# LoRA and paged attention in one kernel: a new order of loads, tables and fillers ahead of the steps, the inverse root ahead of the addition, and queries of step 1 and of the last step turned on TensorE

## The chip, the core and the metric

The kernel runs on one core of one Trainium2 chip. The metric is the device time of one launch in microseconds, as the median of several runs. Beside it stands one execution taken by the hardware profiler, which gives the span from the first to the last instruction and everything that is read from views of the profile.

## The reference, cut to what matters

All data are float32. There are 8 sequences of 128 tokens with 512 features. First each sequence goes through its own adapter weight, and the result is added; then attention over a paged cache is computed on the sum and added again.

```python
x = x + einsum('bsi,boi->bso', x, weight[adapter_ids])     # (8,128,512), adapters 512x512
# attention: 32 query heads, 8 key heads, D = 128, cache of 16 pages x 32 = 512 keys
q = rope(rmsnorm(x @ Wq.T) * q_norm_w)                     # rmsnorm per head
k = rope(rmsnorm(x @ Wk.T) * k_norm_w);  v = x @ Wv.T
scores = q @ [cached keys, k].T / sqrt(D)                  # 512 + 128 keys
scores = where(key number < cache_seqlens (cache part), scores, -1e30)
x = x + (softmax(scores) @ [cached values, v]) @ Wo.T
```

## The kernel before

**Steps.** The work is cut into 32 steps, `steps = [(g, b)]`: four groups g of 8 query heads and 2 key heads, and in each group the 8 sequences b. The projected weights of a group stay in SBUF for its 8 steps. Step i computes 8 heads; for each it does two score matmuls (`sc`, L891, 512 and 128 keys; each shows as two instructions in the profile), a masking and row-minimum operation on VectorE (L901), the exponential on ScalarE (L917), the scaling by the reciprocal on POOL (L966, `p<-p,rc`) and a turn of the probabilities.

**Fillers.** Between two heads, TensorE gets a share of other matmuls from the list `main`: the projections of step i+1 (`project`: `pj_kv`, and `pj_q` for each half of four query heads), `values(i-1, j)` (probabilities times values, `o<-pT`), and `output(i-1)` (`out<-w_o`). In the first group `lora_y` (`y`) and turns of x and of the adapter weight (`lw`) are added. The flag `early` puts the projections ahead of `values(i-1, 0)`; it holds for steps from 8 on. Short TensorE jobs that have a fixed place are in the table `turns_at`, filled with `at(i, head, early, job)`.

**Order.** The order of instructions is the order of the program text (`tc.manual_schedule()`); each engine and each DMA queue runs its own instructions in that order, and semaphores between them are derived from the tiles' buffers. So an instruction that waits holds up all that stand behind it on its engine or queue. SP's queue carries most transfers, ScalarE's queue weights, POOL's queue the gathers of cache pages (`kc`, `vc`) and of adapter weights (`raw_lora`, `lraw`).

**Two ways to turn a matrix.** Through DRAM: VectorE transposes 32x32 blocks, one DMA writes them out and a second reads them back in the right order (`send_q`: `xq<-tq`, then `qT<-xq`; `send_k`/`receive_k`: `xk`, `kT`; `send`/`receive`: `xp`, `pT`; the weights of groups 1 to 3: `xw`, `w`). Or on TensorE: four transposes into a PSUM buffer and a copy out (`turn_q`, `turn_weights`, `turn_x`, `turn_kc`, `turn_lora`). The queries of step 0 are turned on TensorE, those of steps 1 to 31 go through DRAM. PSUM has four buffers for these jobs and for projections (`ps_mm`), and two for scores (`ps_sc`).

**A query half.** When its projection ends, ScalarE takes the squares of its heads (L552), VectorE multiplies by the rotation tables (L557, L561), POOL adds the two products (L568), then adds epsilon to the square sums (L584) and takes the power -1/2 (L585, `rs`); ScalarE scales the four heads with it (L590), VectorE the keys (L593).

**Ahead of the steps.** Loads are issued from SP and ScalarE, the rotation tables are computed with the sine of ScalarE (`rope_tables`, L345 to L385), the row numbers of cache pages on VectorE (`row_numbers`, L278 to L322), and the weights of group 0, x of sequences 0 and 1 and their adapter weights are turned on TensorE, up to the output weights (`wt_o`, 32 transposes). The first score matmul follows.

Of the kernel before, what the change touches and what calls it, by code (L numbers as in the profile page):

```python
# [11 lines left out]
FP = mybir.dt.float32  # L12
# [6 lines left out]
P = 128  # L19
# [33 lines left out]
def lora_then_paged_attention(  # L53
# [51 lines left out]
    def load_x(b, eng=None):  # L105
# [7 lines left out]
    wn = const.tile([P, 2, D], FP, name="wn")  # L113
    nc.scalar.dma_start(out=wn[:, 0, :], in_=q_norm_w.partition_broadcast(P))
    nc.scalar.dma_start(out=wn[:, 1, :], in_=k_norm_w.partition_broadcast(P))
    bt_i = work.tile([P, 4, S], I32, tag="oT0", name="bt_i")
    bt_i = bt_i.rearrange("p a s -> p (a s)")[:, 0 : 4 * B * LC].rearrange("p (c q) -> p c q", q=4)
    nc.scalar.dma_start(
        out=bt_i.rearrange("p c q -> p (c q)"),
        in_=block_table.rearrange("b n -> (b n)").partition_broadcast(P),  # L120
    )
    par = const.tile([P, 1], I32, name="par")
    nc.gpsimd.iota(par, pattern=[[0, 1]], base=0, channel_multiplier=1)
    ident = const.tile([P, P], FP, name="ident")
    make_identity(nc, ident)

    lora_ix = const.tile([P, B], I32, name="lora_ix")
    nc.vector.scalar_tensor_tensor(
        out=lora_ix,
        in0=ids_i,  # L130
        scalar=float(HID // 4),
        in1=par.to_broadcast([P, B]),
        op0=ALU.mult,
        op1=ALU.add,
    )
    lora_rows = lora_w.rearrange("m (p j) i -> (m p) (j i)", j=4)

    def weight_rows(kind, g, n, m=1):  # L140
        if kind == "kv":
            src = wk if n < 2 else wv
            lo = g * GW + (n % 2) * P
            return src[lo : lo + m * P, :]
        if kind in ("q0", "q1"):
            lo = (g * GQ + 4 * int(kind[1])) * D + n * P
            return wq[lo : lo + m * P, :]
        half = int(kind[1])
        lo = (g * GQ + 4 * half) * D
        return wo[n * P : (n + m) * P, lo : lo + 4 * D]  # L150

# [14 lines left out]
    raw = {}  # L166


    first = {}
    for kind, pl, tag in (("kv", turned, "tp"), ("lora", turned, "tp"), ("q0", pts, "pT")):  # L170
        t = pl.tile([P, 4, REP, QK], FP, tag=tag, name=f"raw_{kind}")
        first[kind] = t.rearrange("p a r k -> p (a r k)")[:, 0 : 4 * HID]

    t = wts.tile([P, 4, 4, 4, Q4], FP, tag="o1", name="raw_q1")
    first["q1"] = t.rearrange("p n b c j -> p (n b c j)")

    def load_first(kind, n, m):
        nc.sync.dma_start(
            out=first[kind][:, n * 512 : (n + m) * 512].rearrange("p (n i) -> p n i", n=m),
            in_=weight_rows(kind, 0, n, m).rearrange("(n p) i -> p n i", p=P),  # L180
        )
        for k in range(n, n + m):
            raw[kind, 0, k] = first[kind][:, k * 512 : (k + 1) * 512]

# [10 lines left out]
    for i, (g, b) in enumerate(steps):  # L195
        if i == 0:
            at(i, 1, True, lambda: turn_x1(1))
            at(i, 3, False, lambda: turn_q(0, 1))
        at(i, 2, True, lambda i=i: turn_k(i, 1), 1)
# [18 lines left out]
    for g in range(1, G):  # L218
        before = 8 * B * (g - 1)
        for k, kind in enumerate(("kv", "q0", "q1")):  # L220
            for n in range(4):
                turn_when[before + 9 + 3 * (4 * k + n)] = len(turns_of)
                turns_of.append((kind, g, n))
                h = (2, 3, 5)[k] if g > 1 else (3, 4, 6)[k]
# [18 lines left out]
    load_first("kv", 0, 2)  # L243
    load_first("kv", 2, 2)
    load_first("q0", 0, 4)
    load_x(1)
    load_first("q1", 0, 4)
    load_x(2)

    for k in range(2):  # L250
        for n in range(4):
            t = (acc, x1T)[k][B - 4 + n]
            raw[f"o{k}", 0, n] = t if k == 0 else t.rearrange("p c s -> p (c s)")
            nc.sync.dma_start(out=raw[f"o{k}", 0, n], in_=weight_rows(f"o{k}", 0, n))
# [5 lines left out]
    inner = const.tile([P, 1], FP, name="inner")  # L260
    quad = const.tile([P, 1], FP, name="quad")
    for a in range(4):
        rows = slice(Q4 * a, Q4 * a + Q4)
        nc.gpsimd.iota(
            inner[rows, :],
            pattern=[[0, 1]],
            base=0,
            channel_multiplier=1,
            allow_small_or_imprecise_dtypes=True,
        )  # L270
        nc.gpsimd.memset(quad[rows, :], float(a))
# [3 lines left out]
    def row_numbers():  # L275
# [52 lines left out]
    len_f = const.tile([P, B], FP, name="len_f")  # L328

    key_no = const.tile([P, 4, LC, Q4], FP, name="key_no")  # L330
    nc.gpsimd.iota(
        key_no,
        pattern=[[1, 4], [P, LC], [4, Q4]],
        base=0,
        channel_multiplier=0,
        allow_small_or_imprecise_dtypes=True,
    )
    mhalf = const.tile([P, GQ + GK], FP, name="mhalf")
    nc.gpsimd.memset(mhalf, -0.5)
    masks = [const.tile([P, 4, NC, Q4], FP, name=f"mask_{n}") for n in range(2)]  # L340
    for m in masks:
        nc.gpsimd.memset(m[:, :, LC, :], 0.0)

    def rope_tables():
# [26 lines left out]
        nc.scalar.activation(cos, ang, AF.Abs)  # L371
        nc.vector.tensor_scalar(cos, cos, -1.0, math.pi / 2, ALU.mult, ALU.add)
        nc.scalar.activation(cos, cos, AF.Sin)


        nc.vector.tensor_scalar(wn[:, 0, :], wn[:, 0, :], -SCALE, None, ALU.mult)
# [664 lines left out]
```

## Time and profile before

| | us |
|---|---|
| median of 3 runs | 1244.26 (1242.14 to 1245.38) |
| profiled execution, its time | 1243.9 |
| profiled execution, its span | 1242.1 |
| TensorE matmuls busy | 1193.6 (96%) |
| VectorE busy | 752.9 (61%) |
| POOL busy | 670.5 (54%) |
| ScalarE busy | 527.5 (42%) |
| start to the first score matmul | 57.1 |
| mean granted TensorE clock | 0.986 |

Busy time of an engine is the union of its instructions; register work, waits and the issue of DMAs are not in it. In a row of groups or of the timeline, `out<-in` names the tiles; the bracket behind it gives the idle time of that engine just before the row and what ended it. PE is TensorE's matmul, PEld its weight load, DVE VectorE, ACT ScalarE, SPq and ACTq the issue of a DMA from that queue. The granted clock is a share of full speed.

### The profile page before, as it was taken

The numbers are of one execution on the slowest core, as the hardware profiler recorded it, in microseconds if no ns is written. First come the engines' busy times: TensorE is split into PE (matmuls) and PEld (weight loads), VectorE is DVE, ScalarE is ACT, GpSimd is POOL, SyncE is SP. The second block draws the span as 40 slices with busy tenths as digits, with TensorE's granted clock in tenths as the row PEclk, the third lists the DMA queues.
The fourth block names the chain that finished last, engine by engine and source line by source line (L and its number), as shares of the span: only waits on it lengthen the run. The fifth ranks groups of instructions, "written<-read, shape, count | busy, mean of one in ns | idle before, by whom it ended". The sixth has DMA issues, their size and how long they took to land.

```text
span 1242.1 us, 12908 instructions
## 1 busy us (share of the span) xinstructions
PE 1193.6 (96%) x3380; PEld 579.8 (47%) x3380; DVE 752.9 (61%) x1684; ACT 527.5 (42%) x1643; POOL 670.5 (54%) x763
## 2 busy tenths in 40 slices
PE   6788999999989999999999999999999999999988
PEld 4544444444434444444444444444444444444443
DVE  5264656565646667766666667666666655665731
ACT  3453444444434444444444444443444444444422
POOL 3354464446535566655655566655565556655440
PEclk9898999999999999999999999999999999999989
DMA  7246877786988898888999898888898897777761
GB/s 285 95 151 210 297 256 257 269 286 222 309 275 267 267 334 291 271 296 279 289 346 312 267 342 278 290 277 285 295 352 282 270 299 258 240 263 239 241 223 59
DMA packets 189592, 329.83 MB, mean 266 GB/s; under 512 B 13520, under 2 KB 108112, under 8 KB 180432
## 3 DMA queue, kind: packets, MB, share of 16 engines
q1 hardware_dynamic: 126256, 239.37, 57.6%
q10 hardware_dynamic: 49824, 47.69, 11.9%
q0 software_dynamic: 13440, 41.96, 9.9%
q8 instruction: 27, 0.44, 0.1%
q14 instruction: 45, 0.37, 0.1%
HBM read 196.06 MB, written 132.91 MB: 265 GB/s over the span
## 4 chain that ended last, share of the span: by engine, by line
PE 83%; DMA 10%; DVE 2%; POOL 2%; ACT 1%; issue 1%; ACTq 0%; SPq 0%; DVEq 0%; POOLq 0%
PE sc L891 20%; PE o L474 20%; PE pj_q L474 16%; PE out L474 14%; PE pj_kv L474 8%; DMA qT<-xq 3%; DMA xp<-tp 2%; PE y L474 2%; DMA w_q<-xw_q 2%; DMA xq<-tq 1%; PE lw L397 1%; DMA raw_lora<-in_L_cond_weight_dram,lora_ix 1%; DMA lraw<-in_L_cond_weight_dram,lora_ix 1%; PE x L397 1%; POOL rs L585 1%
## 5 line engine op out<-in xcount | busy, mean ns | idle before, releaser
L901 DVE CUSTOM_DVE_ANT_0 p<-sc,mask 128x640 f32<-128x640 f32 x256 | 210.7, 823 | 350.1 <-PE sc L891 349.5
L891 PE MATMUL sc<-kT,qT 128*128 128x512 f32 (+1 forms) x1024 | 323.5, 439 | 20.5 <-DMA qT<-xq 17.6
L917 ACT ACTIVATE p<-p,mn 128x640 f32<-128x640 f32 x256 | 211.5, 826 | 285.3 <-DVE mn L901 283.2
L891 PEld LDWEIGHTS sc<-kT,qT 128*128 128x128 f32 x1024 | 191.3, 192 | 251.4 <-issue 228.2
L966 POOL TENSOR_SCALAR p<-p,rc 128x640 f32<-128x640 f32 x252 | 201.7, 800 | 193.3 <-DVE rc L959 189.0
L474 PE MATMUL o<-pT,vc 128*128 128x512 f32 x512 | 241.1, 602 | 1.2 <-DMA pT<-xp 1.2
L474 PE MATMUL pj_q<-w_q,x1T 128*128 128x512 f32 x512 | 237.5, 593 | 0.4 <-DMA w_q<-xw_q 0.3
L752 DVE STREAM_TRANSPOSE tp<-p 128x640 f32<-128x640 f32 x252 | 210.7, 836 | 42.3 <-POOL p L966 42.0
L474 PE MATMUL out<-w_o,oT 128*128 128x512 f32 x512 | 235.0, 593 | 0.8 <-ACT oT L726 0.7
L590 ACT ACTIVATE q<-q,rs 128x128 f32<-128x128 f32 x256 | 81.9, 390 | 219.6 <-POOL rs L585 212.5
L520 POOL DMA_INDIRECT kc<-in_L_cond_k_cache_dram,key_ix x128 | 128.9, 1007 | 48.3 <-issue 30.4
L520 POOL DMA_INDIRECT vc<-in_L_cond_v_cache_dram,val_ix x128 | 129.1, 1008 | 35.7 <-issue 31.1
L568 POOL TENSOR_TENSOR q<-q,sw 128x512 f32<-128x512 f32 x64 | 81.8, 1279 | 103.4 <-DVE sw L561 103.1
L474 PEld LDWEIGHTS out<-w_o,oT 128*128 128x128 f32 x512 | 92.7, 190 | 95.7 <-issue 93.5
L474 PEld LDWEIGHTS o<-pT,vc 128*128 128x128 f32 x512 | 93.6, 194 | 92.8 <-issue 84.3
L474 PEld LDWEIGHTS pj_q<-w_q,x1T 128*128 128x128 f32 x512 | 92.5, 191 | 92.3 <-issue 90.1
L474 PE MATMUL pj_kv<-w_kv,x1T 128*128 128x512 f32 x256 | 118.0, 598 | 0.9 <-DVE x1T L399 0.9
L572 POOL TENSOR_TENSOR k<-sw 128x256 f32<-128x256 f32 x31 | 22.9, 740 | 140.8 <-PE kt L653 130.5
L552 ACT ACTIVATE sq<-pj_q 128x128 f32<-128x128 f32 x256 | 70.8, 277 | 48.4 <-PE pj_q L474 39.7
L585 POOL TENSOR_TENSOR rs<-ss,mhalf 128x6 f32<-128x6 f32 x64 | 76.7, 1198 | 5.3
L474 PEld LDWEIGHTS pj_kv<-w_kv,x1T 128*128 128x128 f32 x256 | 46.6, 193 | 46.8 <-issue 45.7
L474 PE MATMUL o<-pT,vn 128*128 128x512 f32 x128 | 65.4, 593 | 0.0
(110 smaller groups left out, 882.5 us busy)
## 6 DMA issues: line engine op xcount, KB each, us to landing
xp<-tp SPq DMA_DIRECT2D x63, 1280.0 KB, 5.7
pT<-xp SPq DMA_DIRECT2D x63, 1280.0 KB, 6.7
xk<-tk SPq DMA_DIRECT2D x31, 512.0 KB, 7.6
kT<-xk SPq DMA_DIRECT2D x62, 256.0 KB, 6.4
xq<-tq SPq DMA_DIRECT2D x62, 256.0 KB, 4.0
qT<-xq SPq DMA_DIRECT2D x62, 256.0 KB, 6.1
st_q<-in_L_cond_Wq_dram ACTq DMA_DIRECT2D x24, 256.0 KB, 4.2
xw_q<-tw_q ACTq DMA_DIRECT2D x24, 256.0 KB, 3.7
```

Of the source, the lines that this page charges most:

```text
L397: nc.tensor.transpose(t[:, j, :], blk, ident)
L474: nc.tensor.matmul(y[0], lhsT=lhsT, rhs=rhs, start=(k == 0), stop=(k == len(pieces) - 1))
L520: nc.gpsimd.indirect_dma_start(out=dst[:, c, :], out_offset=None, in_=src, in_offset=bass.IndirectOffsetOnAxis(ap=rows[:, g, at : at + 1], ...
L552: nc.scalar.activation(sq, t[:, h, :], AF.Square, scale=float(D) ** -0.5, accum_out=ss[:, h : h + 1])
L568: nc.gpsimd.tensor_tensor(dst, dst, sw[:, 0:heads, :], ALU.add)
L585: nc.gpsimd.tensor_tensor(rs[:, 0:width], ss[:, 0:width], mhalf[:, 0:width], ALU.pow)
L590: nc.scalar.activation(q, q, AF.Identity, scale=rs[:, h : h + 1])
L752: nc.vector.transpose(u.tp[:, :, r, :], u.p.pop(r).rearrange("q (a k) -> q a k", a=4))
L891: nc.tensor.matmul(sc[:, lo:hi], lhsT=s.qT[j][:, r, :, :].rearrange("d h q -> d (h q)"), rhs=s.kT[j].rearrange("d a c i -> d (a c i)")[:, ...
L901: nc.vector.tensor_tensor_reduce(out=p, in0=sc[:, 0:LA], in1=masks[i % 2].rearrange("p a c i -> p (a c i)"), scale=1.0, scalar=3.0e38, op0 ...
L917: nc.scalar.activation(p, p, AF.Exp, bias=unit.mn[:, one], scale=-1.0, accum_out=unit.sm[:, one])
L966: nc.gpsimd.tensor_scalar(q, p, unit.rc[:, one], 1.0, ALU.mult, ALU.mult)
```

## The change

It has these parts. (1) **Loads:** the first key/value weights go out first, half from SP and half from ScalarE's queue (there ahead of the page table and norm weights); the weights of the first query half (q0) go from POOL's queue, followed by the adapter weights of sequence 1; the load of q1, those of x and of the output weights wait for a VectorE memset after the angles. (2) **Tables and row numbers:** the constants are made on POOL first; the angles and the sine come before everything else, then the row numbers, then the cosine; two tiny activations (`table_set`) make ScalarE load the sine's and the exponential's tables; the rotation tables for keys and for queries are two calls. (3) **Turns ahead of the steps:** q1's weights are turned in two pairs around the projections, LoRA's turns of sequence 1 use score buffers of PSUM (`spare`), and the eight turns of output weights move into steps 0 and 1. (4) **Root first:** `norm_scales` runs ahead of POOL's addition (`between`). (5) **TensorE turns** the first query half of step 1 and both of step 31; their additions write in the plain order into a buffer of their own. (6) **Steps 6 and 7** become `early`, the second probabilities of steps 5 and 6 use the LoRA buffer, and the weights of group 1 are read one head earlier.

```diff
-    load_first("kv", 0, 2)
-    load_first("kv", 2, 2)
-    load_first("q0", 0, 4)
-    load_x(1)
-    load_first("q1", 0, 4)
-    load_x(2)
...
+    load_first("kv", 0, 2, nc.sync)
+    load_first("kv", 2, 2, nc.scalar)
...
     gather_lora(0, first["lora"])
+    load_first("q0", 0, 4, nc.gpsimd)
+    gather_lora(1)
+
+    def more_loads():
+        nc.vector.memset(first["q1"][:, 0:1], 0.0)
+        load_first("q1", 0, 4, nc.sync)
+        load_x(1)
+        load_x(2)
+        for k in range(2):
+            for n in range(4):
...
+                nc.sync.dma_start(out=raw[f"o{k}", 0, n], in_=weight_rows(f"o{k}", 0, n))
...
         if i == 0:
             at(i, 1, True, lambda: turn_x1(1))
             at(i, 3, False, lambda: turn_q(0, 1))
+            at(i, 7, False, lambda: turn_q(1, 0))
+            for n, h in enumerate((5, 6, 6, 7)):
+                at(i, h, False, lambda n=n: turn_weights(("o0", 0, n)))
+            for n, h in enumerate((7, 8, 9, 10)):
+                at(i, h, False, lambda n=n: turn_weights(("o1", 0, n)))
+        if i == last:
+            at(i - 1, 6, False, lambda: turn_q(last, 0))
+            at(i, 2, True, lambda: turn_q(last, 1))
...
-                h = (2, 3, 5)[k] if g > 1 else (3, 4, 6)[k]
+                h = (2, 3, 5)[k]
                 read_at(before + 8 * (B - 2) + h + n, (kind, g, n))
...
+    def table_set(func):
+        nc.scalar.activation(rope["one"], rope["one"], func)
+    rope["one"] = const.tile([P, 1], FP, name="one")
+    nc.gpsimd.memset(rope["one"], 0.0)
...
+    def rope_cos():
+        cos = rope["cos"]
         nc.vector.tensor_scalar(cos, cos, -1.0, math.pi / 2, ALU.mult, ALU.add)
         nc.scalar.activation(cos, cos, AF.Sin)
+        table_set(AF.Exp)
...
+    by_pe = {(0, 0), (0, 1), (1, 0), (last, 0), (last, 1)}
...
-        if table == 0 or i == 0:
-            nc.gpsimd.tensor_tensor(dst, dst, sw[:, 0:heads, :], ALU.add)
-        else:
+        if between:
+            between()
+        if turned_order:
             nc.gpsimd.tensor_tensor(
                 dst.rearrange("p h (i a) -> p h a i", a=4),
+                cw.rearrange("p h (a i) -> p h a i", a=4),
...
+        else:
+            nc.gpsimd.tensor_tensor(dst, cw, sw[:, 0:heads, :], ALU.add)
...
-            if i:
+            if (i, n) not in by_pe:
                 later.append(lambda: send_q(i, n))
...
-        pl, tag = (lora, "raw") if u.j and u.i >= B - 1 else (pts, "pT")
+        pl, tag = (lora, "raw") if u.j and u.i >= B - 3 else (pts, "pT")
...
+    table_set(AF.Sin)
+    rope_angles()
+    more_loads()
+    row_numbers()
     turn_x(0, on_act)
+    for n in range(4):
+        turn_weights(("kv", 0, n), on_act)
+    rope_cos()
+    rope_table(1)
...
     for c in range(KC):
         turn_lora(0, c, on_act)
     for _, f in lora_y(0):
         f()
     for n in range(4):
         turn_weights(("q0", 0, n), on_act)
     flush()
     turn_x1(0, on_vec)
+    rope_table(0)
+    for n in range(2):
+        turn_weights(("q1", 0, n), on_act)
+    for what in ("kv", "q0"):
+        for _, f in project(0, what):
+            f()
+        run(pending)
+    for n in range(2, 4):
         turn_weights(("q1", 0, n), on_act)
     turn_x(1, on_act)
-    turn_kc(0, 0, on_act)
-    turn_kc(0, 1, on_act)
     for c in range(KC):
-        turn_lora(1, c, on_act if c % 2 else on_vec)
+        turn_lora(1, c, on_act if c < 2 else on_vec, True)
+    for j in range(GK):
+        turn_kc(0, j, on_vec)
+    run(pending)
...
-    for k in range(2):
-        for n in range(4):
-            turn_weights((f"o{k}", 0, n), on_act if n % 2 else on_vec)
...
-        early = i >= B
+        early = i >= B - 2
```

## The prediction

> **What bounds the kernel now.** TensorE is busy for 96% of the span, so I looked for the places where it is not. The first view is a table of stretches, cut at the first score matmul (`sc`, L891) of a step; its columns are length, then busy time of PE, PEld, DVE, ACT and POOL, the granted clock and the DMA.
>
> ```profile
> core 0: us, PE busy (x) PEld busy (x) DVE busy (x) ACT busy (x) POOL busy (x), PEclk, DMA share, GB/s
> 0.00:57.13 57.13, 36.91 (x170) 26.65 (x170) 24.54 (x67) 23.29 (x50) 20.87 (x38) 0.94 0.55 199
> 57.13:95.47 38.34, 32.09 (x103) 16.46 (x103) 20.61 (x49) 20.38 (x63) 19.73 (x23) 0.95 0.44 145
> 95.47:142.11 46.64, 44.72 (x126) 22.43 (x127) 24.89 (x52) 18.67 (x55) 24.15 (x28) 0.90 0.71 238
> 142.11:182.80 40.69, 40.69 (x128) 20.36 (x126) 23.73 (x54) 18.57 (x55) 20.98 (x23) 1.00 0.79 272
> ...
> 307.10:346.95 39.85, 35.50 (x100) 16.52 (x98) 24.02 (x53) 16.92 (x54) 22.59 (x25) 1.00 0.87 285
> 346.95:387.84 40.89, 36.79 (x94) 16.98 (x95) 23.12 (x51) 15.15 (x49) 19.36 (x22) 0.96 0.83 269
> 387.84:424.23 36.39, 36.39 (x94) 17.17 (x95) 23.21 (x51) 15.16 (x49) 20.12 (x24) 0.95 0.79 262
> 424.23:458.86 34.63, 34.63 (x96) 16.40 (x95) 23.75 (x51) 15.04 (x49) 20.52 (x24) 1.00 0.97 319
> ```
>
> Step 2 (from 142.11) and step 9 (from 424.23) have TensorE busy throughout at full clock: 40.69 and 34.63 us are what a step with and without LoRA work costs. Nothing that eases another engine helps there. Time is lost in the start (57.13), in steps 0 and 1, and in steps 6, 7 and 8 (from 307.10, 346.95, 387.84). The second view, TensorE's waits, says on what: six of its idle stretches, and the largest sum, wait for queries that come back from DRAM or for ScalarE's copies.
>
> ```profile
> PE sc L891 <- DMA qT<-xq: 17.6, 5, 5.4
> PE x L397 <- ACT w_q L416: 4.2, 1, 4.2
> ```
>
> The third view is the timeline (start, length, engine, work, idle before it in brackets): on TensorE the end of the start, steps 1, 7, 8 and the last; then ScalarE in the start and in step 0.
>
> ```profile
> 41.78 1.12 PE L397 MATMUL x<-ident,acc 128*128 128x128 f32 x4 [4.22 <-ACT w_q L416]
> 57.13 2.31 PE L891 MATMUL sc<-kT,qT 128*128 128x512 f32 x4 [1.73 <-ACT kT L654]
> 95.47 2.47 PE L891 MATMUL sc<-kT,qT 128*128 128x512 f32 x4 [5.41 <-DMA qT<-xq]
> 346.95 1.95 PE L891 MATMUL sc<-kT,qT 128*128 128x512 f32 x4 [4.28 <-DMA qT<-xq]
> 387.84 1.89 PE L891 MATMUL sc<-kT,qT 128*128 128x512 f32 x4 [2.92 <-DMA qT<-xq]
> 1185.33 2.47 PE L891 MATMUL sc<-kT,qT 128*128 128x512 f32 x4 [4.21 <-DMA qT<-xq]
> 39.98 1.28 ACT L590 ACTIVATE q<-q,rs 128x128 f32<-128x128 f32 x4 [4.58 <-POOL rs L585]
> 60.94 1.28 ACT L917 ACT_TABLE_LOAD   x1
> ```
>
> The four `sc` matmuls that take 1.24 us elsewhere take 1.89 to 2.47 after a gap: a gap costs its length and then a slow stretch, seen as a clock below 1.00 in the table.
>
> **The change, part by part.** Durations are from this one execution: span 1242.1, time 1243.9 (1.8 around the span); the median of the runs is 0.4 above it.
>
> *Start.* The second half of the first key/value weights no longer waits behind the adapter numbers, so it should land near 7 us (it landed at 12.1). I don't count that: ScalarE now runs the sine and its Abs (0.6 each) after the angles, which DVE has at 11.3 as before, and only then copies x and four weight tiles (0.59 each, to 15.5). On DVE the row numbers (4.6) now stand ahead of the cosine, which is therefore ready at 16.4; ScalarE ends it at 17.0, loads the exponential's table (1.28), runs one tiny activation (0.2) and starts the four LoRA copies at 18.5; before they began at 17.65. So `y` of batch 0 ends near 23.5 as before, and `pj_kv` starts at 26.5 (was 26.62). *The rule against this part:* the Trainium skill, ScalarE: Activation LUTs, section "What ACT_TABLE_LOAD costs", gives 1.28 plus a drain of 1.38 for each switch of set. The row above has 1.28 and the exponential starts 0.01 after it, so I take 1.28; by the page everything from here is 1.4 later. The load that disappears from step 0 stood before its first exponential, where TensorE had other work; I count nothing for it.
>
> The gain of the start is behind that. Before, ScalarE's in-order queue held the scaling of the queries (waiting 4.58 for POOL) ahead of the weight copies, and TensorE waited for these (1.89 and 4.22), then did the output weights: 32 transposes from 50.91 to 54.7, 3.8 us. Now: `pj_q` ends at 33.5, squares to 35.2, two weight copies, x and two LoRA copies to 38.0 on ScalarE, the other two and the cached keys on DVE to 40.6; TensorE turns the keys to 39.4, does `y` of batch 1 (3.5 at full clock, up to 5.2 at half), one query turn, and two copies later the first `sc` runs at 44.7 to 46.3. I take 45.5: 11.6 earlier.
>
> The query weights q0 move from SP to POOL's queue, and the second LoRA gather comes before all cache gathers. POOL's nearest row, an indirect load of 128 rows, takes 1.15; 512 rows cost between one such instruction and four (4.6). Behind them stands the memset that the first tiny activation waits for: it falls at 8.7 to 12.1, and only above 11.3 does it delay the sine, by at most 0.8. I take one instruction's cost, so zero.
>
> *Step 0.* The eight output-weight turns (0.43 each) move here (five) and to step 1 (three), and so do their ScalarE copies; TensorE also turns the first queries of step 1 (0.43), which took `xq` 3.7 and `qT` 3.2 through DRAM. In the built program the copy of those queries stands on ScalarE behind the scaling of the *other* four heads, which waits for POOL. POOL's queue from the fifth `p` scaling on, by the rows of before (78.88 to 91.82): `p` 0.8, two key gathers, root and addition 3.0, `p`, two key and two value gathers, 12.9 in all; then scale sum, root and addition 2.7: 94.5. ScalarE: scaling 1.28, exponential 0.8, the query copy 0.57, two weight copies 1.1, key copy 0.4: 98.7, which is 41.6 after the step's first `sc`. Further ahead in the step there is one more delay. Before, scaling (to 73.7), the fourth exponential and a query copy led to the fifth `sc` at 75.04. Now the root is done before the addition, so scaling ends at 72.3; but a value copy (0.37) and two squares (0.8) follow, DVE's key rotation (0.9) waits for these, and then come the mask step (0.83), the exponential (0.83 and 0.2) and the copy (0.57): 76.8, 1.8 later. Step 0 becomes 43.4, 5.1 longer than 38.34. It hides its own five turns (2.2): TensorE has 31.7 of work in it.
>
> *Step 1* is TensorE-bound apart from its first 10 us: three turns, 1.3 longer. *Start to end of step 1: -11.6 + 5.1 + 1.3 = -5.2.*
>
> *Steps 6 to 8.* Steps 6 and 7 now project first and take the values later, as steps 8 to 30 do, with the second `pT` in the LoRA buffer and the new weights read one head earlier. The queries of step 7 are then projected 4.3 (five matmuls of 0.86) earlier. Before, they were sent at 334.66 and landed at 346.8. Now they are sent near 329, but on SP their return stands behind the first `pT`, itself waiting for a landing at 335.2: issued 335.7, landing 7.3 later at 343.0, against 342.2 when TensorE wants them: 0.9 lost. Work: 34.62 three times and one x turn (0.43) = 104.3; steps 14 and 15, which read weights in the same way, lose 1.3 together. 104.3 + 0.9 + 1.3 = 106.5 against 117.1: *-10.6*. Without the new order nothing of it; at best -12.8.
>
> *Root ahead of the addition.* POOL does the same three instructions (1.27, 0.2, 1.04 to 1.35). Squares end before DVE's rotation (1.4), so scale sum and root (1.5) mostly fill POOL's wait; the scaled query comes up to 1.3 earlier. In step 9 `qT` landed at 418.8 for a use at 424.2: 5.5 of cover, so zero.
>
> *Last step.* Both query halves are turned by TensorE: 0.86 for the 4.21 gap and for the slow stretch after it, about 2.6 (the granted clock is 0.50 from 1185.33 to 1190.58). *The rule here:* TensorE: Matmul & The Clock Gate, section "What's actually happening", has the clock halve after an idle window of about 3.4 us; here gaps of 2.92 and 1.73 were followed by slow rows too (1.89 and 2.31 for 1.24). By the page a remaining short gap costs its length alone; by the rows up to 1.7 more. I use the rows: step 0 keeps its slow start. What is late next: `pT` landed at 1184.4, so TensorE waits some 1.7 at 1182.5 instead. Following it head by head, the fourth `sc` of the step comes at 1194.7 for 1199.1: *-4.4*.
>
> Sum: -5.2 - 10.6 - 4.4 = -20.2; 1243.9 - 20.2 = 1223.7, and with the median's 0.4 **1224.0 us**.
>
> **The rivals.** (B) *The start gives nothing:* the POOL chain of step 0, or a slow clock in `y`, takes the 5.2 back: 1229. For it: POOL has 15 us of work in a row there. (C) *The start gives more*: ScalarE isn't held in step 0, which then lasts about 36 instead of 43.4: 1216.6. Against it: the order on ScalarE. (D) *Steps 6 to 8 wait as before*, because the return of the queries stands behind `pT` or the earlier weights land late (7 to 10 us after issue): gain there 2, so 1232.6. (E) *Slower:* the scaling now waits for the addition; if POOL's root waited long for ScalarE's squares, every query would come later. It decides once that lateness exceeds the cover of 5.5 by 20.2/31 = 0.65 per step; 1 us beyond it in 31 steps gives 1224 + 31 = 1255. Against it: squares end before DVE even starts. (F) *No effect*: gaps only move into the next wait, 1243.
>
> **How the numbers follow.** The likeliest case 0.48 (its own range 1217 to 1229), B 0.18, C 0.12, D 0.10, E 0.07, F 0.05. The range 1213 to 1235 leaves out E, F and the far ends of C and D. A measurement of this kernel tells 0.3% (3.7 us) from no change: A to D are faster, 0.88; F 0.05; E 0.07.
>
> **What would show it.** First `sc` near 45.5, of step 1 near 88.9, with ScalarE's scaling in step 0 waiting for POOL; no `qT` wait above 1 us at steps 7, 8 and 31; steps 9 to 29 still 34.62. A step there of over 35.3 would speak for E; a `qT` gap at step 7 for D; a first `sc` after 50 means that the loads or the table work were on the path.

## The result

The changed kernel takes 1229.93 us (median of four runs, 1229.44 to 1230.35) against 1244.82 before (four runs, 1242.14 to 1250.2: the three above and one more): a ratio of 0.9875, 95% interval 0.9842 to 0.9908. It is faster, by 15 us where 20 were forecast. The profiled executions are 1230.35 (span 1228.5) and 1243.9 (span 1242.1). The table of stretches after the change, cut where a step's first `sc` (now L953) starts; columns are length, busy time of PE, PEld, DVE, ACT and POOL, granted clock, DMA share and rate:

```profile
core 0: us, PE busy (x) PEld busy (x) DVE busy (x) ACT busy (x) POOL busy (x), PEclk, DMA share, GB/s
0.00:44.16 44.16, 31.00 (x138) 20.70 (x138) 22.55 (x66) 19.29 (x46) 22.92 (x39) 0.92 0.67 239
44.16:86.57 42.41, 34.69 (x126) 18.66 (x126) 20.69 (x51) 23.03 (x72) 23.65 (x28) 0.94 0.41 143
86.57:133.97 47.40, 45.41 (x139) 23.58 (x140) 24.08 (x51) 18.90 (x54) 21.54 (x25) 0.91 0.70 234
296.71:336.59 39.88, 35.50 (x100) 16.72 (x98) 25.20 (x53) 16.74 (x54) 21.42 (x24) 1.00 0.90 296
336.59:372.97 36.38, 36.38 (x94) 17.22 (x95) 22.18 (x51) 15.16 (x49) 19.71 (x22) 0.95 0.88 282
372.97:407.60 34.63, 34.63 (x96) 16.41 (x95) 22.27 (x51) 15.27 (x49) 21.17 (x25) 1.00 0.84 285
1165.98:1228.50 62.52, 53.42 (x146) 24.89 (x144) 14.75 (x34) 15.46 (x33) 16.65 (x17) 0.94 0.32 110
```

The rows are the start, steps 0, 1, 6, 7, 8 and the last step. Steps 7 and 8 keep TensorE busy throughout; step 6 still has 4.4 us of idle TensorE, step 0 has 7.7 and the last step 9.1. TensorE's three largest waits in the steps (releaser, then total, times, longest):

```profile
PE kt L708 <- ACT qT L718: 4.8, 1, 4.8
PE o L509 <- DMA pT<-xp: 4.2, 1, 4.2
PE sc L953 <- DMA qT<-xq: 3.7, 1, 3.7
```

In place of five waits and 17.6 us for queries from DRAM there is one, and one for probabilities. The timeline says where (start, length, engine, work, idle before it):

```profile
44.16 1.35 PE L953 MATMUL sc<-kT,qT 128*128 128x512 f32 x4 [0.86 <-ACT kT L709]
82.72 1.28 ACT L637 ACTIVATE q<-q,rs 128x128 f32<-128x128 f32 x4 [4.00 <-POOL q L624]
84.72 0.56 ACT L718 COPY qT<-qt 128x512 f32<-128x512 f32 x1
85.34 0.47 PE L708 MATMUL kt<-ident,k 128*128 128x128 f32 x1 [4.78 <-ACT qT L718]
336.59 1.67 PE L953 MATMUL sc<-kT,qT 128*128 128x512 f32 x4 [3.71 <-DMA qT<-xq]
1165.98 1.24 PE L953 MATMUL sc<-kT,qT 128*128 128x512 f32 x4
1188.12 2.93 PE L509 MATMUL o<-pT,vc 128*128 128x512 f32 x3 [4.24 <-DMA pT<-xp]
```

So the first `sc` is at 44.16; the end of step 0 waits, on ScalarE, for POOL; step 7 still waits for its queries; and the last step starts without a gap but has one in its middle. The balance in the two profiled executions, from the starts of the steps:

| stretch | before | after | difference | forecast |
|---|---|---|---|---|
| to the first `sc` | 57.13 | 44.16 | -13.0 | -11.6 |
| step 0 | 38.34 | 42.41 | +4.1 | +5.1 |
| step 1 | 46.64 | 47.40 | +0.8 | +1.3 |
| step 4 | 42.85 | 40.69 | -2.2 | 0 |
| steps 6 to 8 | 117.14 | 110.87 | -6.3 | -10.6 |
| steps 14, 15, 22, 23 | 140.36 | 141.57 | +1.2 | 0 |
| steps 30 and 31 | 88.90 | 90.72 | +1.8 | -4.4 |
| span | 1242.1 | 1228.5 | -13.6 | -20.2 |

One caution for all that follows. Eleven executions of kernels that share the changed kernel's start have their first `sc` between 43.95 and 47.18. The traces show where they part: from the first `pj_kv` to the first `sc` they all take 17.62 or 17.63, but VectorE's copy of the turned x, which `pj_kv` reads, begins 0.04 us after the turn in some and up to 2.7 us after it in others. What holds the copy the traces do not name. After a late start step 0 is some 1.4 shorter, because the slow clock stretch behind its 2.00 gap is absent there (last section), so its end moves less: 86.5 to 88.2. For one kind of start step 0 repeats well: 42.41 and 42.44 in two early executions without an edit in it, 41.05 to 41.07 in four late ones. Steps 30 and 31 do not: ten executions with the changed kernel's end take 86.2 to 90.8, mean 89.0.

The kernel before, measured again beside each variant, had medians of 1241.8 to 1244.8, so the ratio to it is given with each time; the 95% intervals reach 0.2 to 0.4% to either side, and by ratio only three variants are clear of the changed kernel (0.9875): the first queries of step 1 through DRAM, the root behind the addition, and the three together. So I read the step that an edit touches, against executions with the same start, more than the medians.

### The profile page after: what moved, and what is told of

It is laid out like the page before. It is cut to its first block, busy times and chain, and to the rows that moved or that the text cites. A ratio compares the mean times of both kernels' runs of the same rounds, so it can differ in the third digit from the quotient of the medians.

```text
span 1228.5 us, 12918 instructions
## 1 busy us (share of the span) xinstructions
PE 1190.2 (97%) x3392; PEld 578.0 (47%) x3392; DVE 733.7 (60%) x1681; ACT 529.8 (43%) x1649; POOL 672.1 (55%) x765
## 4 chain that ended last, share of the span: by engine, by line
PE 88%; DMA 6%; POOL 2%; ACT 2%; issue 1%; DVE 1%; ACTq 0%; DVEq 0%; POOLq 0%; SPq 0%
PE sc L953 21%; PE o L509 21%; PE pj_q L509 17%; PE out L509 16%; PE pj_kv L509 9%; PE y L509 2%; DMA xp<-tp 2%; DMA w_q<-xw_q 2%; PE lw L431 1%; DMA raw_lora<-in_L_cond_weight_dram,lora_ix 1%; DMA qT<-xq 1%; DMA pT<-xp 1%; PE x L431 1%; PE kt L708 0%; POOL vc L556 0%
## 5 line engine op out<-in xcount | busy, mean ns | idle before, releaser
L953 PE MATMUL sc<-kT,qT 128*128 128x512 f32 (+1 forms) x1024 | 321.6, 437 | 9.2 <-DMA qT<-xq 3.7
L953 PEld LDWEIGHTS sc<-kT,qT 128*128 128x128 f32 x1024 | 190.8, 191 | 238.2 <-issue 212.4
L624 POOL TENSOR_TENSOR q<-q,sw 128x512 f32<-128x512 f32 x61 | 77.0, 1262 | 46.8 <-DVE sw L608 46.8
```

What stands on the lines that cost most here:

```text
L624: nc.gpsimd.tensor_tensor(dst, cw, sw[:, 0:heads, :], ALU.add)
L953: nc.tensor.matmul(sc[:, lo:hi], lhsT=s.qT[j][:, r, :, :].rearrange("d h q -> d (h q)"), rhs=s.kT[j].rearrange("d a c i -> d (a c i)")[:, ...
```

## The experiments

Each is the changed kernel with one edit; the last one combines three.

**Steps 6 and 7 in the old order.**

```diff
-        early = i >= B - 2
+        early = i >= B
-        pl, tag = (lora, "raw") if u.j and u.i >= B - 3 else (pts, "pT")
+        pl, tag = (lora, "raw") if u.j and u.i >= B - 1 else (pts, "pT")
-                h = (2, 3, 5)[k]
+                h = (2, 3, 5)[k] if g > 1 else (3, 4, 6)[k]
```

> Steps 6 and 7 take values first again, the second half's probabilities come back into their old buffer, and the weights of group 1 are read at heads 3, 4 and 6 again; the rest is the changed kernel. If this part is worth what the two traces show for steps 6 to 8 (117.1 us before, 110.9 after), the time rises by 6.2, to 1236, with TensorE's waits for queries (some 4.3 and 2.9) back at the first scores of steps 7 and 8. If it is worth what the forecast gave (10.6), and something else in the changed kernel took the rest away again, it rises to 1240. If the steps gained from another part (shorter start, other phase of the transfers), it rises by under 2.

1234.45 us (1229.24 to 1238.71, six runs), ratio to before 0.9926 (0.9901 to 0.9951). In the profiled execution steps 6 to 8 take 39.14 + 39.76 + 34.70 = 113.6, 2.7 more than after the change (110.9, which is also the mean of the nine executions that keep the new order unedited there; they range from 110.1 to 113.5); TensorE waits for queries at both places:

```profile
PE sc L953 <- DMA qT<-xq: 6.2, 2, 3.7
```

The 3.7 at step 7 stands with the old order as with the new one; only the second wait (2.46, at step 8) comes back. So the part removes the wait of step 8 and not that of step 7. Its size is not settled: 2.7 by the steps, where the range of the new order reaches almost to this one execution of the old one, and 6.3 by the ratios, whose intervals overlap and are 3 to 4 us wide to either side. The forecast's 10.6 is above both. And even with the old order these steps take 3.5 less here than before the change (117.1), which this part does not explain.

**Only the weight reads of group 1 back** (the last pair of lines of the diff above alone).

> Only the reads of group 1's weights go back from heads 2, 3 and 5 to heads 3, 4 and 6; the new order of steps 6 and 7 stays. Theory 1: the queries of step 7 come late in the changed kernel (7.63 us to DRAM and 9.71 back, where before it was 4.75 and 7.34) because these reads now fall into the same stretch. Then the two transfers shrink by some 2 us or more together, and the wait of 3.71 at the first score of step 7 falls to under 2; the key/value weights, issued one head (4.6 us) later, may then be what TensorE waits for at the start of step 7, up to 4. Theory 2: the DMA is full in that stretch with what is moved anyway (share 1.01 at 335 GB/s); the wait stays at 3 to 4, and the time within 1 us of 1230, or later if weights are late.

1232.76 us (1230.41 to 1233.03), ratio 0.9901. The first `sc` of step 7 waits 5.08, for 3.71. The queries go out at 321.50 and their return is issued at 328.51, so the way to DRAM still took about 7.0, and the semaphore of the return is full at 340.14, 11.6 after the issue. Theory 1 falls: it is not these reads, moved by one head, that make the transfers long.

**TensorE turns the queries of step 7.**

```diff
-    by_pe = {(0, 0), (0, 1), (1, 0), (last, 0), (last, 1)}
+    by_pe = {(0, 0), (0, 1), (1, 0), (B - 1, 0), (last, 0), (last, 1)}
+        if i == B - 1:
+            at(i - 1, 7, False, lambda: turn_q(B - 1, 0))
```

> TensorE also turns the first query half of step 7 (four transposes, 0.43 us at full clock, at the end of step 6), so that these queries don't go through DRAM. If the 3.71 us wait at step 7 is that transfer alone, step 6 goes from 39.87 to 36.6 or less, the slow stretch after it (337.4 to 340.8 at half clock, some 1.7 lost) goes too, and the time is 1225 to 1227. If the wait is only the first of several late transfers (cached keys, weights; these take 8.8 and 9.8 us there), it moves to the next of them, and under 1 us is gained.

1230.43 us (1229.11 to 1231.39), ratio 0.9885; no gain. The transposes run at 333.37, but the copy of their result does not follow. ScalarE's timeline:

```profile
332.60 0.19 ACT L981 ACTIVATION_READ_ACCUMULATOR p<-p,mn 128x1 f32 x1
337.19 0.37 ACTq L476 DMA_DIRECT2D w_q<-xw_q  x1
337.60 0.59 ACT L720 COPY qT<-qt 128x512 f32<-128x512 f32 x1 [4.82 <-DMA pT<-xp]
```

A weight read that ScalarE has to issue goes out only at 337.19, and the copy stands behind it: the wait moved from the DMA queue of the queries into ScalarE's queue, 4.26 on TensorE. The bracket names what the issue waits for: `pT`, issued on SP's queue at 326.43 and landed at 337.17. By the trace the weight read uses the same semaphore as that transfer (the DMAs of both queues share eight), and it waits until the earlier transfer has filled it. In the changed kernel the DMA engines are all busy there (share 1.01 at 337 GB/s from 315 to 337), and taking the two transfers of these queries out did not help.

**Values of the last step gathered in the last step.**

```diff
-                if h in (5, 6):
+                if h in (5, 6) and i + 1 < last:
                     gather_v(i + 1, 2 * h - 10)
                     gather_v(i + 1, 2 * h - 9)
+            if i == last and h in (0, 1):
+                gather_v(i, 2 * h)
+                gather_v(i, 2 * h + 1)
```

> The four gathers of cached values for the last step are issued in the last step (heads 0 and 1) and no longer in the step before (heads 5 and 6), where the first waits 5.24 us on POOL for a buffer that the last value matmuls of that step free. Theory: POOL's order makes the last steps wait; behind that gather stand the root and addition of the last queries and two scalings of probabilities, so the second half's probabilities of step 30 leave late (1175.65), land at 1188.08, and TensorE waits 4.24 for them and then runs 6.8 at half clock. Then they leave 4 to 6 us earlier, the wait goes or falls under 1, and the time is 1223 to 1226. Rival: the two transfers of these probabilities themselves (5.1 and 7.2) or the vector transposes set the time; then the time stays within 1 of 1230.

1223.22 us (1221.01 to 1226.77), ratio 0.9835. The last step takes 54.68 for 62.52 (58.0 to 62.6 in the ten executions with the changed kernel's end), with no wait for `pT` above 0.5. POOL in the changed kernel, and then here:

```profile
1159.53 0.80 POOL L1028 TENSOR_SCALAR p<-p,rc 128x640 f32<-128x640 f32 x1 [2.71 <-DVE rc L1021]
1165.57 1.11 POOL L556 DMA_INDIRECT vc<-in_L_cond_v_cache_dram,val_ix  x1 [5.24 <-PE o L509]
...
1170.58 0.79 POOL L1028 TENSOR_SCALAR p<-p,rc 128x640 f32<-128x640 f32 x1
...
1173.93 0.81 POOL L1028 TENSOR_SCALAR p<-p,rc 128x640 f32<-128x640 f32 x1
```

```profile
1164.80 0.79 POOL L1028 TENSOR_SCALAR p<-p,rc 128x640 f32<-128x640 f32 x1
1167.24 0.80 POOL L1028 TENSOR_SCALAR p<-p,rc 128x640 f32<-128x640 f32 x1 [1.65 <-DVE rc L1021]
```

The gather waits for a buffer that the last value matmuls in step 30 read; the scalings of `p` stand behind it. Without it they come 6 to 7 us earlier, and the second half's `xp` leaves at 1169.12 for 1175.65. It is POOL's order, then, and not the transfer.

**Queries of the last step through DRAM** (the two `last` entries of `by_pe` and their `turn_q` calls removed).

> Both query halves of the last step go through DRAM again, as before the change; everything else is the changed kernel. If the turn by TensorE only moved the wait (steps 30 and 31 took 88.93 us before and 90.76 after), the time falls by about 1.8, to 1228, with the wait for queries of about 4 back at the first score and the one for probabilities gone. If the turn is worth what the forecast gave, and something else in the changed kernel makes the end late, the time rises by up to 4.4, to 1234.

1227.6 us (1226.95 to 1228.79), ratio 0.9890. Steps 30 and 31 take 30.37 + 56.16 = 86.5, against 90.7 after the change and 86.2 to 90.8 in the ten executions with its end. The gap at the first `sc` is back (2.45), the one at `pT` is gone. So the turn alone brings nothing that can be seen here; it moves the wait. What it is worth once the gathers are late, no run shows: none has late gathers and queries through DRAM.

**Values of step 1 gathered in step 1.**

```diff
-                if h in (5, 6):
+                if h in (5, 6) and i:
+            if i == 1 and h in (0, 1):
+                gather_v(1, 2 * h)
+                gather_v(1, 2 * h + 1)
```

> The four gathers of cached values for step 1 are issued in step 1 (heads 0 and 1) and no longer in step 0 (heads 5 and 6); they are needed in step 2. Theory: POOL's queue sets the end of step 0: root and addition of the second query half stand behind two of these gathers (77.81 to 80.00), ScalarE waits 4.00 for them, and the query and key copies that step 1 needs stand behind that scaling. Then the first score of step 1 comes 2 to 2.5 earlier (84.2 for 86.57) and the time is near 1227.6. Rival: the squares or VectorE's products are ready only then, or the cached keys land no earlier; then under 0.5 is gained.

1224.66 us (1223.45 to 1228.86), ratio 0.9878, by which nothing is gained; the steps show it. The start is that of the changed kernel (43.95); step 0 takes 39.88 for 42.41, 2.5 less, and step 1 0.8 less. The second addition of queries runs on POOL at 78.68 for 81.44. So POOL's queue did hold the end of step 0.

**The turns for step 1 one head earlier** (`turn_q(1, 0)` and `turn_k(1, 0)` at head 6 of step 0).

> In step 0 the turn of the first queries of step 1 and the turn of its new keys go from head 7 to head 6, so that ScalarE's copies of them stand ahead of the scaling of the other query half, which waits 4.00 for POOL. Theory: it is ScalarE's order that passes POOL's lateness on to TensorE. Then the first score of step 1 follows the last work of step 0 (80.6 for 86.57), and the time falls by 3 to 6, to 1224 to 1227; less than the 6 if step 1 waits a little later for the same scaling (exponential of the eighth head at 83.91). Rival: step 1 waits for its cached keys or its probabilities then; under 1 is gained.

1222.96 us (1220.45 to 1224.6), ratio 0.9848. Here the copies of queries and keys run at 77.97 and 79.77, ahead of the scaling, which still waits 2.84 for POOL until 83.00, and no longer delays TensorE:

```profile
77.97 0.57 ACT L718 COPY qT<-qt 128x512 f32<-128x512 f32 x1
83.00 1.28 ACT L637 ACTIVATE q<-q,rs 128x128 f32<-128x128 f32 x4 [2.84 <-POOL q L624]
```

Step 0 takes 37.03 after a start at 45.84; an unedited step 0 with nearly that start (45.75) took 41.07. So 4 of the forecast 3 to 6 in this step, by the order on ScalarE.

**First queries of step 1 through DRAM** (`(1, 0)` taken out of `by_pe`, with its `turn_q`).

> The first query half of step 1 goes through DRAM again; the rest is the changed kernel. It is scaled at 75.5; with 0.9 for the vector transpose and its wait, 3.7 to DRAM and 3.2 back it would land near 84.5, ahead of the key copy on ScalarE, which ends at 86.52 and would end 0.6 earlier without the query copy. By this the turn brings nothing at step 1: first score near 86.0, time 1229 to 1230. If the transfers take as long as in the changed kernel's step 6 (7.6 and 9.7), the queries land near 94, step 1 begins 7 later and the time is 1236 to 1237.

1233.92 us (1232.24 to 1235.01), ratio 0.9938. Step 0 takes 45.68 from the same start, 3.3 more, with a wait of 9.61 on TensorE:

```profile
89.81 2.47 PE L952 MATMUL sc<-kT,qT 128*128 128x512 f32 x4 [9.61 <-DMA qT<-xq]
```

Neither of my two figures: `xq` was sent at 79.68, some 2 later than in my sum, because the vector transpose stands behind the rotation of the other half; its return was issued 5.6 later and landed 4.5 after that. The turn by TensorE is worth 3.3 in this step.

**Output weights turned ahead of the steps, as before.**

```diff
-            for n, h in enumerate((5, 6, 6, 7)):
-                at(i, h, False, lambda n=n: turn_weights(("o0", 0, n)))
-            for n, h in enumerate((7, 8, 9, 10)):
-                at(i, h, False, lambda n=n: turn_weights(("o1", 0, n)))
...
+    for k in range(2):
+        for n in range(4):
+            turn_weights((f"o{k}", 0, n), on_act if n % 2 else on_vec)
```

> The eight turns of output weights go back ahead of the steps, their copies by turns on ScalarE and VectorE; the rest is the changed kernel. By the forecast's working (32 transposes, 3.8 us, hidden in step 0) the first score comes 3.8 later (48.0 for 44.16); step 0 has 4.78 of idle TensorE at its end which the turns no longer fill, and it is shorter only by two weight copies (1.1) that stand ahead of the key copy on ScalarE. Time 1232.6 to 1233.7. Rival: the cached keys, root and scaling of the first queries are late enough that the turns fit into a wait ahead of the first score; then under 1.5 is lost.

1222.03 us (1216.93 to 1225.48), ratio 0.9833: *faster* than the changed kernel, by 8 in the medians and 5 by the ratios, where 3 slower was expected. The first `sc` is at 50.51, 22.47 after `pj_kv` for 17.62, so 4.9 later by the turns. But step 0 then takes 31.30 for 42.41 and step 1 44.88 for 47.40:

```profile
50.51:81.81 31.30, 30.21 (x106) 15.88 (x106) 19.15 (x47) 19.66 (x63) 17.15 (x20) 1.00 0.48 172
81.81:126.69 44.88, 41.20 (x126) 20.41 (x127) 25.60 (x54) 18.38 (x55) 26.86 (x31) 1.00 0.77 256
```

ScalarE at the end of step 0 shows why:

```profile
80.89 0.59 ACT L714 COPY qT<-qt 128x512 f32<-128x512 f32 x1 [0.36 <-issue]
81.38 0.39 ACT L705 COPY kT<-kt 128x128 f32<-128x128 f32 x1
88.69 1.28 ACT L633 ACTIVATE q<-q,rs 128x128 f32<-128x128 f32 x4 [6.93 <-POOL q L620]
```

The program spreads the fillers evenly over the heads that are left. Fewer turns in step 0 make the share of each head smaller, so the second projection of queries ends one head later; its scaling then stands *behind* the copies that step 1 needs. It waits for POOL even longer (6.93), and nothing on TensorE waits with it. This is the order that the edit with earlier turns makes too; here the filler copies are out of the way as well.

**Root behind the addition again.**

```diff
-        if between:
-            between()
...
+        if between:
+            between()
```

> On POOL the addition of the two query products comes ahead of scale sum and root again. The forecast put this part at zero, with 5.5 us of cover in the steps. Time 1230 within 1. Rival: where POOL's chain is on the path (end of the start, steps 0 and 1, steps 7 and 31) scaled queries come up to 1.3 later in each place; then 1232 to 1234.

1240.54 us (1234.53 to 1244.44, 20 runs), ratio to before 0.9973 (0.9955 to 0.9991). This is the largest of the single edits: without the root first, the other parts together gain 0.3%. Its steps, and below them those of an execution with the same start (47.13) and root first, that with the late values above:

```profile
47.04:90.80 43.76, 33.54 (x127) 18.05 (x127) 22.57 (x51) 23.02 (x72) 24.39 (x28) 0.95 0.40 143
90.80:139.52 48.72, 45.78 (x139) 23.46 (x139) 24.36 (x52) 18.98 (x55) 22.41 (x26) 0.91 0.71 234
...
303.81:345.83 42.02, 35.75 (x99) 16.77 (x98) 23.89 (x53) 16.82 (x54) 22.32 (x25) 1.00 0.86 285
```

```profile
47.13:88.19 41.06, 33.00 (x127) 18.07 (x127) 21.04 (x51) 23.02 (x72) 23.68 (x28) 0.97 0.42 148
88.19:135.14 46.95, 44.97 (x139) 23.43 (x140) 24.07 (x51) 18.89 (x54) 21.54 (x25) 0.92 0.69 234
298.45:337.56 39.11, 35.49 (x99) 16.70 (x98) 25.15 (x53) 16.73 (x54) 21.36 (x24) 1.00 0.90 296
```

Steps 0, 1 and 6 are 2.7, 1.8 and 2.9 longer, 7.4 together; of step 6 up to 2 may be chance, since it took 39.1 to 41.2 in the other kernels with its new order. The medians are 10.6 apart; 2.2 of that lies between this profiled execution (1238.37) and the median, and where the rest comes from is open. In step 6 the first queries of step 7 leave 24.05 after the step's start, for 22.34 in the changed kernel, and TensorE waits 5.07 for them.

**The exponential's table loaded in step 0** (`table_set(AF.Exp)` left out).

> The tiny activation that loads the exponential's table during the start is left out; the load falls before the first exponential of step 0, as before the change. By the row of the trace (1.28 us, the next operation 0.01 after it) and 0.2 for the activation, the LoRA copies and the first score come up to 1.5 earlier (42.7 for 44.16)[...]. In step 0 the first exponential comes 1.28 later, where TensorE has other work for 4 us. If step 0 is held by POOL later on, it ends 1.5 earlier too, and the time is 1228.5; if loads from DRAM and not ScalarE set the start, the time stays at 1230.

1230.11 us (1226.35 to 1232.17), ratio 0.9895. The first `sc` is at 44.10, no earlier. `y` of batch 0 ends 0.8 earlier, at 22.5, and the sum of x and `y` is turned at 24.81 for 25.66 (25.4 to 27.3 in the other variants), but VectorE's copy of it begins 0.83 after the turn, for 0.04 in the changed kernel, and `pj_kv` starts at 26.48 for 26.54. So some 0.8 of the load was won and lost again in the delay that differs from execution to execution; what the load costs at the first `sc`, this one trace does not settle. In step 0 the load costs 1.28 with no pause behind it:

```profile
46.52 1.28 ACT L978 ACT_TABLE_LOAD   x1
47.82 0.83 ACT L978 ACTIVATE p<-p,mn 128x640 f32<-128x640 f32 x1
```

**Three together:** output weights ahead, values of step 1 and of the last step late.

> Three edits of the changed kernel together: the eight output-weight turns ahead of the steps (alone: step 0 of 31.30 with TensorE busy throughout, for 42.41), the cached values of step 1 gathered in step 1, and those of the last step gathered in the last step (alone: last step 54.7 for 62.5). If the gains stand in separate places they add: 1222.0 and 1223.2 are 7.9 and 6.7 below the changed kernel, together 1215, and 0 to 2 less by the gathers of step 1, since POOL holds ScalarE there for 6.9 while TensorE waits 1.7 for LoRA rows that are gathered behind them: 1213 to 1216. Rival: a step that starts earlier only waits for transfers at a later place (steps 4, 6, 14, 22), and half is given back: 1219 to 1222.

1212.52 us (1209.64 to 1216.49, six runs), ratio to before 0.9753 (0.9728 to 0.9778): faster than both kernels. By the medians the gains add as expected:

```profile
0.00:48.81 48.81, 34.43 (x169) 23.93 (x170) 26.10 (x71) 21.64 (x50) 24.13 (x40) 1.00 0.61 220
48.81:80.11 31.30, 30.21 (x106) 15.88 (x107) 19.52 (x47) 19.66 (x63) 17.44 (x21) 1.00 0.49 171
80.11:124.81 44.70, 42.69 (x127) 21.08 (x128) 24.92 (x54) 18.62 (x55) 26.77 (x30) 0.96 0.75 258
1158.19:1213.40 55.21, 50.09 (x146) 23.91 (x144) 14.42 (x34) 14.10 (x29) 13.76 (x13) 1.00 0.36 126
```

Start, step 0, step 1 and the last step: 180.0 for 196.5 in the changed kernel. Step 1 ends at 124.81, 1.9 earlier than with the output weights ahead alone, so most of the late values' own 3.6 there (133.97 to 130.41) is covered by the other edit. The longest wait left in the steps is step 7's for its queries, 4.10 here.

## Why the prediction was right or wrong

**The start: right, its first part by another path.** -13.0 for -11.6; over the eleven executions -10.0 to -13.2. `pj_kv` starts at 26.54, where I had 26.5. But the chain of work that leads to it in this trace does not run over ScalarE's sine and table load. It runs over the LoRA rows, which landed at 15.96, and their turns on TensorE, to 19.54, a path that I had not counted:

```profile
16.10 3.64 PE L431 MATMUL lw<-ident,raw_lora 128*128 128x128 f32 x16 [1.72 <-DMA raw_lora<-in_L_cond_weight_dram,lora_ix]
```

In the variant with steps 6 and 7 in the old order the chain is the forecast one, over the table load. So the two paths end close together, and without the load only some 0.8 was won ahead of the turn of x. From `pj_kv` on the chain is the forecast one (squares, two weight copies, x, LoRA copies, cached keys, `y`), and its 17.6 us lie just under my 18.2 to 19.8. On the weighed rule of the Trainium skill, ScalarE: Activation LUTs, section "What ACT_TABLE_LOAD costs": with 1.28 in the row and the next operation 0.01 to 0.02 behind it in three loads, no drain of 1.38 is seen. No run takes the new order of loads and of q1's turns back, so that the waits for weight copies are gone is read from the two traces, and how the 13 us divide is not shown.

**Step 0: right in size and in mechanism, wrong in one term.** 42.41 for 43.4, with ScalarE's scaling waiting for POOL; both the edit on POOL's queue (2.5) and the one on ScalarE's order (4) shorten it as that chain says. The term that failed is "It hides its own five turns (2.2)". TensorE hides them, but they push the second projection one head forward and so put the waiting scaling ahead of the copies. With the turns ahead, step 0 ends at 81.8 and step 1 at 126.7; with them inside, at 86.5 to 88.2 and 133.9 to 135.4. They cost 5 to 6 by the end of step 0 and 7 to 9 by the end of step 1, where I had a gain of 3.8 without a price. Of this the order on ScalarE is shown alone (4); the rest goes with fewer turns and copies in both steps. Smaller terms were off too: the fifth `sc` of step 0 came 1.0 later than before and not 1.8.

**Step 1: right** (+0.8 for +1.3). **Step 4** gained 2.2 that I had not looked for: two short waits for LoRA rows and queries of before are absent. In the other kernels with this order step 4 takes 41.1 to 42.1, so half of it and more may be chance.

**Steps 6 to 8: the mechanism half right, the size off.** The queries did leave 5.2 earlier in the step (22.3 after its start, before 27.6). SP's rows, after the change and before it:

```profile
318.45 0.33 SPq L826 DMA_DIRECT2D xp<-tp  x1
319.05 0.32 SPq L754 DMA_DIRECT2D xq<-tq  x1
325.06 0.37 SPq L835 DMA_DIRECT2D pT<-xp  x1
326.74 0.36 SPq L761 DMA_DIRECT2D qT<-xq  x1
```

```profile
329.36 0.33 SPq L770 DMA_DIRECT2D xp<-tp  x1
334.66 0.32 SPq L698 DMA_DIRECT2D xq<-tq  x1
335.31 0.37 SPq L779 DMA_DIRECT2D pT<-xp  x1
339.47 0.37 SPq L705 DMA_DIRECT2D qT<-xq  x1
```

I had "issued 335.7 behind the first `pT`, landing 7.3 later". The issue of the return was not held by `pT`; instead the way out took 7.63 (before 4.75) and the way back 9.71 (before 7.34), so that the queries landed 39.7 after the start of the step in both kernels. The mis-sized term is the transfer time. Two things differ: the stretch is somewhat fuller (337 GB/s for 315), and the queries now stand close behind the 1280 KB of probabilities on the same queue. `xq` left 0.6 after `xp`, for 5.3 before, and landed 1.8 after it; `qT` left 1.7 after `pT`, for 4.2, and landed 2.0 after it. Which of the two made the transfers long, no run separates. The wait at step 8, on the other hand, is gone as forecast, and steps 7 and 8 have no idle TensorE.

**Root ahead of the addition: "5.5 us of cover, so zero" was wrong.** I had worked out the gain (up to 1.3 per query half) and then looked for its cover in step 9. Steps 0, 1 and 6 have none, and step 0 has two halves in one chain. The part is worth 4.5 to 7.4 in these steps, and without it the balance above would be smaller by that much. A piece of it was in my chain for step 0 (scaling ends 1.4 earlier there), but not as a term of its own. That the total came within 6 us is luck to this extent: a part counted at zero made up for others that gave less than forecast.

**The last step: 4.4 forecast, no gain seen.** Steps 30 and 31 took 88.9 before, 90.7 in this execution and 89.0 in the mean of ten. Up to the fourth `sc` the forecast held: it comes 40.3 after the start of step 30, for 45.9 before. For what is late next I went no further than "`pT` landed at 1184.4, so TensorE waits some 1.7 at 1182.5", the first half's. That wait didn't come. The step of the forecast that failed is this look ahead. What is late next is the *second* half's `pT`, and it is late through POOL's gather. Before the change the same gather waited 4.57, but the gap for queries left that `pT` time to spare (it landed at 1202.20 for a use at 1204.68):

```profile
1180.55 1.11 POOL L520 DMA_INDIRECT vc<-in_L_cond_v_cache_dram,val_ix  x1 [4.57 <-PE o L474]
```

So 5.6 were won by the fourth `sc`, and 4.24 of wait and about 3.4 of the slow stretch behind it (6.8 us at half clock) lost after it.

**Rivals.** B and C named step 0 as the place to gain or lose; both edges were there to be had (31.3 was possible) but the order decided against C, as argued. D was half true: step 7 waits as before, step 8 doesn't. E did not come: steps 9 to 13 take 34.62 as before. F was true of the last step alone.

## What to carry to other kernels

Look for an in-order queue that waits for a buffer or for another engine, and list what stands behind it on that queue: three edits that put gathers on POOL, a waiting scaling and weight copies on ScalarE behind or out of the way of what TensorE needs next gave 17 us here in the medians, 15 by the ratios. When work is moved into a planned step as filler, compare the order of every engine before and after, because the filler shifts what stands around it. A cover is to be looked for in every stage in which the instruction runs, and when a wait is removed, the next two landings are to be followed, not one.

## What the hardware showed that was not expected

The granted clock went to half after gaps that are shorter than the window of about 3.4 us that the Trainium skill, TensorE: Matmul & The Clock Gate, section "What's actually happening", gives. With the queries of the last step through DRAM, a gap of 2.45 was followed by four matmuls in 2.35, for 1.24 at full clock. Yet length alone doesn't decide: a gap of 2.00 ahead of the fifth `sc` of step 0 was followed by 3.4 us of half clock in the changed kernel (64.3 to 67.8), and by none with the turns one head earlier (clock 1.00 over the whole step).

What decides can be worked out from the granted clock in the traces. In each execution all half-clock stretches begin on a grid of 3.413 us: in the changed kernel at 13.14, 64.34, 84.82, 337.41 and 1187.33, which is 15, 21, 95 and 344 grid steps after the first. There the gap of 2.00 lies in one interval of the grid (60.93 to 64.34), with TensorE busy for 41% of it; with the turns one head earlier it is divided over two, busy for 81% and 60%. I counted such intervals in all 14 traces, from 45 us to shortly before the end. Of intervals at full clock, half clock followed all 37 in which TensorE's matmuls were busy for under 40%, 7 of 9 between 40 and 50%, and none of 4697 above. An interval at half clock was followed by another in all 31 cases under 79%, and by full clock in all 44 above. So in these traces idle time of under half an interval (1.7 us in one interval) cost its length alone; more cost a slow stretch or not by where the grid fell, and that differs from execution to execution. A forecast has to carry the slow stretch behind a gap of 2 to 3 us as a range.

On SP's queue, in the traces before and after, all 498 transfers that were issued while the one ahead was still under way landed after it. A 256 KB transfer of queries took 6.1 and 6.4 us in the median when probabilities were under way just ahead of it, and 2.8 and 3.0 with nothing under way; the DMA was also fuller in the first case (median share 0.96 and 0.97, for 0.58 and 0.63), so the two causes are not separated. Either way a landing taken from one stretch does not carry into another in which the queue holds something else.
